# Layer 1's deferred steps: one in each tile of keys, in place of up to four ahead of each burst of weighted sums

## The chip, the cores and the metric

One core of a Trainium2 chip runs the whole program in one launch. The time is device microseconds of one execution, from the first instruction to the last; beside it the profiler's span of one profiled execution is given. Engines are named as the profile names them: PE is TensorE (matrix products), PEld its weight loads, DVE is VectorE, ACT is ScalarE, POOL is GpSimd, SP is the engine that issues most of the DMAs.

## The reference

Two layers, each a cross attention and a gated or routed feed-forward part, on x of 4 batches x 512 rows x 256 columns and a context of 4 x 1601 x 256, all in float32. The part that matters here is layer 1's attention, with 16 heads of 16 columns, and the routing that follows it:

```python
def _L1_xattn_ref(q, k, v, mask, wq_w, wq_b, wk_w, wk_b, wv_w, wv_b, fo_w, fo_b):
    qp = (q @ wq_w.T + wq_b).reshape(N, -1, HEADS, HEAD_DIM)
    kp = (k @ wk_w.T + wk_b).reshape(N, -1, HEADS, HEAD_DIM)
    vp = (v @ wv_w.T + wv_b).reshape(N, -1, HEADS, HEAD_DIM)
    energy = jnp.einsum('nqhd,nkhd->nhqk', qp, kp)
    energy = jnp.where(mask == 0, jnp.float32(-1e+20), energy)
    attention = jax.nn.softmax(energy / np.float32(np.sqrt(EMBED)), axis=3)
    out = jnp.einsum('nhql,nlhd->nqhd', attention, vp).reshape(N, -1, EMBED)
    return out @ fo_w.T + fo_b
...
x = x + _L1_xattn_ref(_layernorm(x, axis=-1), ctx_1024, ctx_1024, mask_Bx1xSxS2_ik1, ...)
x = x + _L1_ffn_ref(_layernorm(x, axis=-1), L1_ffn_gate_weight, L1_ffn_gate_up_proj, L1_ffn_down_proj)
```

The feed-forward part `_L1_ffn_ref` takes the softmax of 32 gate logits for each row, keeps the 8 largest, gives every row a place in the buffers of its 8 experts, and sums the experts' outputs by their shares.

## The kernel before, in words

The program runs layer 0 (`xattn0`, `ffn0`), then layer 1's attention (`xattn1_keys`, line 1150; another form, `xattn1`, is there for general masks and does not run with this input), then the experts (`experts1`). The change touches the attention and the norm that it shares with others.

**Slots and tiles.** `xattn1_keys` works through 16 slots (line 1404). A slot is one batch b and one group g of four heads. In a slot, the loop at line 1414 goes over NK = 13 tiles of 128 keys (the last has 65). For each tile and each of the four heads s, TensorE multiplies 128 keys with 512 queries (line 1428, tile `sb`, 32 rows of the array, row group s), and ScalarE takes the exponential into `pt` (line 1433).

**Maxima.** The scores need each query's maximum ahead of time. The generator `maxima` (line 1270) works one slot ahead: each `next(top)` runs `maximum` (line 1135), two products of 32 rows (line 1143, tile `sa`) into one of two double banks, and one VectorE reduction (line 1146, `mx`). The loop asks for 32/26 of them at every second head (lines 1419 to 1423). After the fourth maximum of a slot, `rows` (line 1288) transposes the slot's maxima and sends them to the row of `qs` that the scores read.

**Weighted sums.** The exponentials are kept in 23 buffers. After tiles 2, 5, 8, 10 and 12 the held tiles are put on a list, and two tiles later `burst` (line 1391) takes them off and calls `weigh` (line 1353): for each tile and head a product of the values with the exponentials, 32 columns of the array each, four heads side by side (line 1361). The sum is added into `ov` by VectorE (line 1369), or copied by ScalarE for the first (line 1367).

**Deferred steps.** All else is cut into steps by `yield` and waits on the list `more`; `step` (line 1297) runs the next piece of the list's first generator. They are:
- `project(b)` (line 1202): loads the context, takes the norm of x, adds the output's bias to x, then (after `yield True`) two steps of transposes, eight steps of key chunks (line 1223, stored to `kd` in memory through two buffers `kc`) and two of queries (line 1234, to `qd`).
- `values(b)` (line 1244): 13 steps, one for each tile of keys, of a product (line 1251) and a VectorE add into `v1` (line 1255).
- `normalise(i, ov)` (line 1306): transposes a slot's sums and divides them. It is put at the list's head when a slot's last burst has run.
- `finish(b)` (line 1325): the output projection in four steps, then the router's `route_steps` (line 1617): norm, transposes, logits, top 8, positions, and for each of four row tiles a step that builds one-hots (lines 1705 to 1718) and one that multiplies them (line 1725).

Before, a step is run in `burst` alone: up to four, ending early at a `yield True`, ahead of the weighted sums. Two other places run steps where something must be ready: line 1409 empties the list when batch 1 or 2 begins, and line 1276 runs steps until the projection that `maxima` needs is done.

**Banks and order.** Scores `sb`, the steps' products and the weighted sums all take turns in four PSUM banks (tag "s" of `ps_s`); the maxima have the other four, two pairs (`ps_a`). The order of the work on every engine is the order written (`tc.manual_schedule`, line 1371): an engine that waits holds back what is behind it.

**The norm.** `layernorm` (line 91) calls `moments` (line 95: eight VectorE instructions for four row tiles, and a square root on ScalarE) and `normed` (line 107: a reciprocal and four VectorE instructions). It is used by `project` and `route_steps`, where it ran as one piece.

## Time and profile before

| what | us |
|---|---|
| time, median of 3 runs (lowest, highest) | 2245.74 (2242.94, 2249.98) |
| the profiled execution's time | 2245.39 |
| its span | 2243.6 |
| layer 0, up to some 1003 us | about 1003 |
| layer 1's attention, first scores to the last weighted sum | 1008.3 to 1944.1 |
| routing of the last batch, then the experts | to the end |
| PE busy from 1100 to 1900, in each 100 us | 94 to 97 |
| DVE busy in the same stretches | 60 to 77 |
| ACT busy in the same stretches | 47 to 56 |
| weighted sums, 12 products of 512 columns (one burst of three tiles) | 2.71 |
| row work of tiles 1 to 3, 4 to 6, 7 to 9 in a slot without steps | 8.37, 7.52, 8.11 |
| VectorE reduction `mx`, mean | 0.989 |
| exponential `pt`, mean | 0.604 |

How to read it: the profile lists, for one execution, how long each engine was busy, in which stretches, and what ended each of its idle times. In a stretch's line the columns are its limits in us from the span's start, its length, and the busy time of PE, PEld, DVE, ACT and POOL with the number of instructions in brackets, then the TensorE clock that was granted (1.00 is full) and the load of the DMA engines. In a line of instructions, the count and the mean come after the shapes; what stands behind the last bar is the idle time of that engine just before them and who ended it.

### The profile page before, as it was taken

To read this page: it belongs to the slowest core of one execution; us is meant where nothing else is said; L and a number is where in the kernel's file an instruction comes from. 1 tells how busy PE (TensorE), PEld (TensorE's weight loads), DVE (VectorE), ACT (ScalarE), POOL (GpSimd) and SP (SyncE) were. 2 spreads that over 40 slices of the span, in tenths; PEclk is the share of its full clock that TensorE was granted. 3 is DMA by queue.
4 is the path that set the end of the run, shared out by engine and by line. 5 is a ranking of instruction groups with operands and counts; after the bars stand their busy time and mean duration, and the time that the engine had idled before them with its cause. 6 is when DMAs were issued, how large, how long until landed. Compare 5 with 4: busy or idle time off the path is not lost.

```text
span 2243.6 us, 29693 instructions
## 1 busy us (share of the span) xinstructions
PE 2069.1 (92%) x11446; PEld 1071.0 (48%) x11446; DVE 1183.3 (53%) x1916; ACT 736.0 (33%) x1543; POOL 772.4 (34%) x769
## 2 busy tenths in 40 slices
PE   6999999999999999989999999999999999859883
PEld 4677744444444543334444344444444444446551
DVE  5343346445555444656567667875677675232220
ACT  1221222112112121104545545554455555512121
POOL 9999445555444445531000000000000000037764
PEclk9999999999999999999999999999999999959996
DMA  6473121121122223133212222123122200037763
GB/s 212 134 257 101 44 78 48 49 64 50 51 61 68 57 73 75 53 66 70 72 33 35 69 47 47 29 57 66 28 37 33 42 11 11 19 107 184 166 146 38
DMA packets 98190, 161.89 MB, mean 72 GB/s; under 512 B 20100, under 2 KB 68760, under 8 KB 97528
## 3 DMA queue, kind: packets, MB, share of 16 engines
q1 hardware_dynamic: 79800, 126.00, 21.8%
q0 software_dynamic: 17664, 33.38, 7.3%
q8 instruction: 93, 1.52, 0.3%
q14 instruction: 57, 0.47, 0.1%
q10 hardware_dynamic: 576, 0.52, 0.1%
HBM read 137.28 MB, written 22.31 MB: 71 GB/s over the span
## 4 chain that ended last, share of the span: by engine, by line
PE 48%; DVE 8%; DMA 5%; issue 3%; POOL 1%; ACT 1%; POOLq 0%; ACTq 0%; SPq 0%; DVEq 0%
PE sb L1428 12%; PE sa L1143 10%; PE pv L1361 7%; DVE mx L1146 4%; DMA out<-eo,ids 4%; PE acc L561 3%; PE py L857 2%; PE pv L1251 2%; PE po_e L1507 2%; PE pk L1223 2%; PE gu L1491 1%; POOL out L1519 1%; PE pf L1342 1%; PE ph L1725 1%; DMA qd<-kc 1%
## 5 line engine op out<-in xcount | busy, mean ns | idle before, releaser
L1146 DVE TENSOR_REDUCE mx<-sa 128x2 f32<-128x802 f32 x512 | 494.5, 989 | 158.9 <-PE sb L1428 83.9
L1433 ACT ACTIVATE pt<-sb 128x512 f32<-128x512 f32 (+1 forms) x832 | 429.7, 605 | 277.2 <-PE sb L1428 253.0
L1143 PE MATMUL sa<-kq,qq 32*128 32x401 f32 x2048 | 475.0, 550 | 31.2 <-DVE mx L1146 25.2
L1143 PEld LDWEIGHTS sa<-kq,qq 32*128 32x128 f32 x2048 | 175.8, 189 | 202.1 <-DVE mx L1146 167.6
L1718 POOL TENSOR_TENSOR r_hold<-r_lb,r_pr 128x256 f32<-128x256 f32 x16 | 10.1, 629 | 684.1 <-DVE r_lb L1711 559.7
L1428 PE MATMUL sb<-b 32*128 32x512 f32 (+1 forms) x832 | 233.8, 657 | 10.5 <-ACT pt L1433 7.4
L561 PE MATMUL acc<-og,oe 128*128 128x512 f32 x512 | 239.7, 598 | 2.4 <-DVE og L542 2.4
L857 PE MATMUL py<-ve,xnT 128*128 128x512 f32 x512 | 231.7, 595 | 3.3 <-DVE mx L1146 3.2
L1428 PE MATMUL sb<-qs,ks 32*128 32x512 f32 (+1 forms) x832 | 226.2, 641 | 4.0 <-ACT pt L1433 3.5
L1361 PE MATMUL pv<-pt,v 128*32 128x512 f32 (+1 forms) x1664 | 196.1, 597 | 0.0
L862 DVE TENSOR_TENSOR y<-py,gm 128x1024 f32<-128x1024 f32 x64 | 78.3, 1224 | 209.2 <-PE py L857 152.4
L499 POOL TENSOR_SCALAR pr<-pr,den 128x128 f32<-128x128 f32 (+3 forms) x128 | 143.7, 1133 | 123.3 <-DVE den L497 123.3
L871 POOL TENSOR_TENSOR y_a<-y 128x512 f32<-128x512 f32 x64 | 81.5, 1273 | 247.7 <-DVE den L497 147.1
L488 ACT ACTIVATE pr<-sc,nm 128x128 f32<-128x128 f32 (+3 forms) x128 | 66.3, 523 | 280.1 <-DVE nm L484 177.8
L857 PEld LDWEIGHTS py<-ve,xnT 128*128 128x128 f32 x512 | 95.5, 190 | 118.0 <-issue 112.3
L561 PEld LDWEIGHTS acc<-og,oe 128*128 128x128 f32 x512 | 91.1, 190 | 90.3 <-issue 85.5
L1428 PEld LDWEIGHTS sb<-b 32*128 32x128 f32 (+1 forms) x832 | 89.2, 188 | 88.0 <-issue 34.3
L1428 PEld LDWEIGHTS sb<-qs,ks 32*128 32x128 f32 (+1 forms) x832 | 87.7, 182 | 81.7 <-issue 36.1
L1519 POOL DMA_INDIRECT out<-eo,ids x64 | 101.4, 1585 | 57.2 <-ACT eo L1513 36.7
L542 DVE TENSOR_TENSOR og<-gb,oT 128x512 f32<-128x512 f32 x128 | 114.6, 935 | 0.5
L1369 DVE TENSOR_TENSOR ov<-pv,ov 128x512 f32<-128x512 f32 x64 | 44.1, 688 | 121.2 <-PE pv L1361 120.5
L227 PE MATMUL sc<-ctxT,qT 128*128 128x512 f32 (+1 forms) x256 | 96.3, 527 | 7.3 <-ACT pr L239 7.3
(262 smaller groups left out, 2659.1 us busy)
## 6 DMA issues: line engine op xcount, KB each, us to landing
gb<-gd SPq DMA_DIRECT2D x128, 256.0 KB
mi<-in_mask POOLq DMA_DIRECT2D x32, 401.0 KB, 3.7
wgu<-in_E_gu SPq DMA_DIRECT2D x32, 384.0 KB
qq<-qd SPq DMA_DIRECT2D x64, 128.0 KB
kq<-kd SPq DMA_DIRECT2D x64, 100.2 KB
ctxT<-in_ctxT SPq DMA_DIRECT2D x8, 800.5 KB
ctxT<-in_ctxT SPq DMA_DIRECT2D x12, 512.0 KB
ctx<-in_ctx SPq DMA_DIRECT2D x12, 512.0 KB
```

The costliest lines, as they stand in the source:

```text
L227: nc.tensor.matmul(sc[:, c : c + n], qT[:, m, t * P : (t + 1) * P], ctxT[b][j][:, m, :n], start=(m == 0), stop=(m == 1),)
L499: nc.gpsimd.tensor_scalar(pr[:, j, :n], pr[:, j, :n], den[:, j : j + 1], None, ALU.mult)
L542: nc.vector.tensor_tensor(og, gb[:, i, :], oT[s], ALU.mult)
L561: nc.tensor.matmul(acc[b][m], oe[hp][:, c : c + P], og, start=(hp == 0 and e == 0), stop=(hp == NP - 1 and e == E0 - 1),)
L857: nc.tensor.matmul(py[:, j, :], xnT[:, k, t * P : (t + 1) * P], ve[:, k, j, :], start=(k == 0), stop=(k == 1),)
L871: nc.gpsimd.tensor_tensor(a, yy[:, :, :h4], yy[:, :, h4:], ALU.add)
L1143: nc.tensor.matmul(pa[:, j, :Q1], qq[r, s, t * P : (t + 1) * P], kq[r, s, :], start=True, stop=True)
L1146: nc.vector.tensor_reduce(mx[:, t, s, 2 * half : 2 * half + 2], pa[:, :, :Q1], AX.X, ALU.max)
L1361: nc.tensor.matmul(pv[32 * s : 32 * s + 32, :], v1[b % 2][:r, kt, h * VW : h * VW + 32], pts[s][:r, :], start=(kt == held[0][0]), stop=(kt ...
L1428: nc.tensor.matmul(sb[:r, :], ks[i % 2][q, kt * P : kt * P + r], qs[i % 2][q, :], start=True, stop=True,)
L1433: nc.scalar.activation(pt[:r, :], sb[:r, :], AF.Exp)
L1519: i = nc.gpsimd.indirect_dma_start(out=view, out_offset=bass.IndirectOffsetOnAxis(ap=router.ids[:, e, c : c + 1], axis=0), in_=eo[:, c, :] ...
```

## The change

The norm becomes a generator of four steps (`layernorm_steps`, `moments_steps`), used by `project` and `route_steps`; `moments` runs the same pieces at once for the other callers. `burst` no longer runs steps. In the loop over tiles, one step is run at the third head of every tile, after the maxima asked for there and ahead of that head's scores; a second one is run at the first head in every tile of slot 0 and in tile 1 of every other slot, ahead of the burst if one is due there. Steps that ended a burst's run of steps by `yield True` no longer differ from the others. The instructions and their operands stay as they were; their order changes.

```diff
--- before.py
+++ after.py
@@ -92,16 +92,38 @@
 
         return self.normed(b, pool, *self.moments(b, pool))
 
+    def layernorm_steps(self, b, pool, xn):
+
+        nc = self.nc
+        mv, rstd = yield from self.moments_steps(b, pool)
+        nc.vector.reciprocal(rstd, rstd)
+        xn.append(pool.tile([P, TB, D], F32, name="ln_xn"))
+        for t in range(TB):
+            self.normed_tile(b, t, xn[0], mv, rstd)
+            if t % 2:
+                yield
+
     def moments(self, b, pool):
 
+        steps = self.moments_steps(b, pool)
+        while True:
+            try:
+                next(steps)
+            except StopIteration as e:
+                return e.value
+
+    def moments_steps(self, b, pool):
         nc = self.nc
         mv = pool.tile([P, TB, 2], F32, name="ln_mv")
         for t in range(TB):
+            if t == 2:
+                yield
             st = pool.tile([P, 6], F32, name="ln_st")
             nc.vector.bn_stats(st, self.xs[b * TB + t])
             nc.vector.bn_aggr(mv[:, t, :], st)
         rstd = pool.tile([P, TB], F32, name="ln_rstd")
         nc.scalar.activation(rstd, mv[:, :, 1], AF.Sqrt, bias=self.eps)
+        yield
         return mv, rstd
 
     def normed(self, b, pool, mv, rstd):
@@ -109,11 +131,14 @@
         nc.vector.reciprocal(rstd, rstd)
         xn = pool.tile([P, TB, D], F32, name="ln_xn")
         for t in range(TB):
-            nc.vector.tensor_scalar(
-                xn[:, t, :], self.xs[b * TB + t], mv[:, t, 0:1], rstd[:, t : t + 1],
-                ALU.subtract, ALU.mult,
-            )
+            self.normed_tile(b, t, xn, mv, rstd)
         return xn
+
+    def normed_tile(self, b, t, xn, mv, rstd):
+        self.nc.vector.tensor_scalar(
+            xn[:, t, :], self.xs[b * TB + t], mv[:, t, 0:1], rstd[:, t : t + 1],
+            ALU.subtract, ALU.mult,
+        )
 
     def transposed(self, xn, pool, ps, tag):
 
@@ -1202,7 +1227,9 @@
             def project(b):
 
                 ctxT = ctx[b] = self.load_context(b, p1)
-                xn = self.layernorm(b, p1)
+                xn = []
+                yield from self.layernorm_steps(b, p1, xn)
+                (xn,) = xn
                 add_bias(b)
                 kd[b] = dram.tile([D, S2], F32, name="kd")
                 qd[b] = dram.tile([D, S], F32, name="qd")
@@ -1389,9 +1416,6 @@
                 ov = {}
 
                 def burst():
-                    for _ in range(4):
-                        if step():
-                            break
                     _, i, some = bursts.pop(0)
                     if some[0][0] == 0:
                         ov[i] = p2.tile([P, S], F32, name="ov")
@@ -1421,6 +1445,8 @@
                                 while due >= 1:
                                     next(top, None)
                                     due -= 1
+                            if s == 2 or (s == 0 and (i == 0 or kt == 1)):
+                                step()
                             if s == 0 and bursts and bursts[0][0] + 2 <= now:
                                 burst()
                             q = slice(32 * s, 32 * s + 32)
@@ -1618,7 +1644,9 @@
 
         nc, prog = self.nc, self.prog
         sh = [P, TB, E1]
-        xn = prog.layernorm(b, p1)
+        xn = []
+        yield from prog.layernorm_steps(b, p1, xn)
+        (xn,) = xn
         for t in range(b * TB, (b + 1) * TB):
             nc.sync.dma_start(prog.out[t * P : (t + 1) * P, :], prog.xs[t])
         nc.sync.dma_start(
```

## The prediction

> **What bounds the kernel now.** I read the page first, then stretches of the layer 1 attention cut at its slots (one slot is one batch and one group of four heads, 13 tiles of keys), then stretches cut where TensorE changes its kind of work, and last the order of time around one full-array product that already sits among the row-tiled ones.

> ```profile
> span 2243.6 us, 29693 instructions
> PE 2069.1 (92%) x11446; PEld 1071.0 (48%) x11446; DVE 1183.3 (53%) x1916; ACT 736.0 (33%) x1543; POOL 772.4 (34%) x769
> L1146 DVE TENSOR_REDUCE mx<-sa 128x2 f32<-128x802 f32 x512 | 494.5, 989 | 158.9 <-PE sb L1428 83.9
> L1433 ACT ACTIVATE pt<-sb 128x512 f32<-128x512 f32 (+1 forms) x832 | 429.7, 605 | 277.2 <-PE sb L1428 253.0
> ```

> The page: TensorE is busy nearly throughout, while VectorE's maxima (0.99 us each) and ScalarE's exponentials wait for it. A slot needs 32 maxima and 52 exponentials. "Busy" does not mean full: a row-tiled product uses a quarter of the array.

> ```profile
> core 0: us, PE busy (x) PEld busy (x) DVE busy (x) ACT busy (x) POOL busy (x), PEclk, DMA share, GB/s
> 1202.57:1250.95 48.38, 46.56 (x348) 19.63 (x344) 35.29 (x45) 28.76 (x55) 0.00 (x0) 1.00 0.23 35
> 1250.95:1328.76 77.81, 72.90 (x424) 34.59 (x420) 43.91 (x64) 35.11 (x65) 2.98 (x4) 0.96 0.27 67
> 1328.76:1391.77 63.01, 60.20 (x404) 29.43 (x401) 43.69 (x67) 32.26 (x61) 0.00 (x0) 0.97 0.22 42
> 1391.77:1446.34 54.57, 52.11 (x430) 22.76 (x427) 43.12 (x81) 29.02 (x56) 0.63 (x1) 0.97 0.17 30
> 1446.34:1496.99 50.65, 48.90 (x540) 22.55 (x536) 39.18 (x53) 30.27 (x58) 1.89 (x3) 1.00 0.21 33
> ```

> Five slots, the second column the length. The first is quiet: almost no deferred step runs in it, 48.38 us. The next four carry one batch's steps: keys and queries first (77.81), values (63.01), outputs and the router's norm (54.57), the rest of the routing (50.65). Their excess over quiet is 29.4 + 14.6 + 6.2 + 2.3 = 52.5 us per batch. This is what the change can win or lose; the quiet part stays.

> ```profile
> 1323.26:1326.91 3.65, 3.65 (x19) 2.96 (x17) 2.28 (x5) 0.98 (x3) 0.00 (x0) 1.00 0.01 1
> 1250.95:1265.57 14.62, 10.97 (x61) 5.35 (x57) 11.32 (x19) 8.53 (x15) 2.98 (x4) 0.77 0.26 104
> 1415.33:1424.44 9.11, 9.10 (x57) 4.53 (x53) 8.48 (x23) 5.56 (x11) 0.00 (x0) 1.00 0.10 25
> 1235.30:1241.49 6.19, 5.86 (x44) 2.84 (x40) 4.18 (x5) 3.94 (x8) 0.00 (x0) 1.00 0.65 67
> 1243.35:1249.10 5.75, 4.86 (x40) 2.42 (x37) 4.50 (x5) 3.12 (x7) 0.00 (x0) 1.00 0.33 88
> ```

> In order: four value steps in one burst (3.65 us, so 0.91 each); the row-tiled stretch in which a whole norm ran (8.37 in the quiet slot, so 6.25 more); the one in which the router's top-8 ran (8.11 quiet, so 1.0 more); and two stretches of two tiles each, the first with the transposes of the maxima (line 1291, called from line 1282) in its middle, the second without.

> ```profile
> 1238.51 0.60 PE L1291 MATMUL tp_m<-ident,nm 128*4 128x128 f32 x4
> 1239.03 1.43 PE L1428 MATMUL sb<-qs,ks 32*128 32x512 f32 x7
> 1239.99 0.52 PE L1143 MATMUL sa<-kq,qq 32*128 32x401 f32 x3
> 1240.88 1.89 DVE L1146 TENSOR_REDUCE mx<-sa 128x2 f32<-128x802 f32 x2 [1.27 <-PE sb L1428]
> ```

> That is a step of the kind that the change makes: full-array work alone among row-tiled work. It takes 0.53 us of TensorE's order (1238.51 to 1239.03), and VectorE then idles 1.27 us before its next maximum.

> **The change, part by part.** *What it moves.* Before, a burst ran up to four steps and then its weighted sums; five bursts a slot. After, a step runs at the second pair of heads of every tile, and one more in tile 1: 14 a slot, 26 in slot 0. One batch needs 17 (projection, its norm now four more) + 13 (values) + 4 (normalise) + 22 (outputs and routing, again four more) = 56 = 4 x 14, so the drain at line 1409 finds the queue empty and nothing piles up there. The number of products, copies and DMAs is unchanged. SP gets the same issues in nearly the same order; keys' stores come one per tile instead of four per burst.

> *Full-array steps* (52 values, 24 key chunks, 6 queries, 12 norm and router transposes and logits, 12 of the output: 106). In a burst each cost its TensorE time: stretches after stepped bursts are as long as after quiet ones (7.56 against 7.52 for tiles 4 to 6). Among row-tiled work, two score banks feed VectorE, and its maxima start 1.02 us apart (8 in 8.22 us): one maximum frees a bank, TensorE refills it in about 0.94 us, and the other maximum has then just ended. There is almost no slack, so a step that sits between two refills delays the next maximum by its own length. Bounds from the transposes above: 6.19 - 5.75 = 0.44 for 0.53 us, so 0.09 under par; VectorE's idle of 1.27 against its usual 0.14 is 1.13, so 0.6 over. The second is the nearer for a step whose following score products take the row groups that the next refill wants (the refill at 1239.99 starts when the second passes of 1239.57 end); by the count of 32/26 maxima per half tile this holds for every other step, and part is regained because both banks are then free. I take par, 0, with ends -0.09 x 106 = -10 and +0.6 x 106 = +64. The results' copies to SBUF fall into the idle time that the step makes, as they did in bursts.

> [...] The row: the first transpose starts 0.44 us after the last refill's second pass began, that is, at once when it has streamed, and the scores follow 0.2 us after the last transpose starts. [...]

> *VectorE's own steps.* Norms and routing have little TensorE work; in a burst VectorE did them while TensorE multiplied (2.48 of 2.71 us in the burst after the top-8), and now they stand in the chain of maxima. I charge each its time less 0.25 (maxima at 0.91 back to back instead of 1.02, 2.46 a tile), and nothing where the next thing is a burst.
> - The router's norm: 2 x (0.425 + 0.182) = 1.2, 1.2, 1.2 (reciprocal and two tiles at 0.51) and 1.0, less 1.0 = 3.6; ScalarE's square root with table loads of 1.28 there and back holds the exponentials, 1.5 of it felt: 5.1. Before, 2.8 (8.55 against 5.75). +2.3.
> - The projection's norm: 5.1 less 1.2, since its second piece stands just ahead of tile 1's burst: 3.9. Before 6.25. -2.3.
> - Top-8 and what goes with it: 4.2 (eight small ones a tile group, from 0.09 to 0.29) less 0.25 = 3.9; before 1.0. +2.9.
> - Slots and one-hots: 1.8 + 4 x (1.215 + 0.417) + 4 x 0.28 = 9.4; the two one-hots at tiles 9 and 11 go under bursts (-3.3), 1.2 off for seven steps; plus four small products at 0.6: 7.3. Before, 2.65 in its stretch and 4 x 0.62: 5.1. +2.2.

> Batches 1 and 2: +5.1 each. Batch 3 has routing alone (its norm cost 4.1 before, 10.25 against 6.19, and 4.5 now): +5.4. Batch 0 has a projection alone (4.1 before, 9.87 against 5.75, and 3.9 now): -0.2. Together +15. Ends: -5 if bursts go on hiding most of it, +35 if no burst hides any and ScalarE's stalls count whole.

> *Small parts.* Bursts with four key chunks waited for the two store buffers: 5.79 against 3 x 1.72 + 0.25 = 5.4, six times, -2; weighted sums waited for the last value's copy, 3.0 in all, -3. Normalise: its VectorE part (0.25 + 4 x 0.215 = 1.1) lay under the burst, now beside 0.59 of TensorE; +0.15 x 15 = +2. Start: the first value step stands ahead of the first scores (1008.3) and needs 1.6 MB of context whose issue begins at 1003.5; at the 355 to 384 GB/s of 1005 to 1009 that lands near 1009, the bias row later: +2 (0 to 4).

> Sum: 0 + 15 - 5 + 2 + 2 = +14 on the profiled execution's 2245.4 (span 2243.6 and 1.8 around it), which is the median of the runs, 2245.7, to 0.4 us. **2259 us.**

> **The rivals.** *Faster, 2217 us:* steps fill TensorE's waits for VectorE. For it: unhindered, TensorE issues a tile's row work in 1.85 us (1202.57 to 1204.42) where the tile takes 7.52 / 3 = 2.51; 0.66 is left a tile, and if 0.4 of it takes up step work in 106 tiles, that is 2245.4 + 14 - 42. Against: that slack is in pieces on single row groups, and a full-array product needs all four free. It decides from 0.13 us hidden per step. *Much slower, 2323:* every step meets the 0.6 us of the upper bound, +64 beside the +14; for it the 1.27 us of idle, against it the parity that frees every other step. *No change, 2245:* par for the products, and routing's VectorE work still hidden (end of -5 with +5 of the rest).

> **How the numbers follow.** The forecast (some 2252 to 2290) 0.44, much slower 0.14, no change 0.14, faster 0.28. Slower by over 0.3% (7 us, about what this kernel's measurement can tell): 0.44 + 0.14 = 0.58; within it 0.14; faster 0.28. The likeliest case's own range is 2252 to 2290; the range 2215 to 2305 reaches into both rivals so that about one in ten is left out on either side.

> **What would show it.** Right: slots with keys and values keep about 77 and 63 us, those with routing grow by some 5 in all, VectorE idles about 1 us after each step, and quiet slots stay at 48.4. Wrong: a tile with a value step takes under 3.2 us on average (2.5 + 0.9 less 0.2), so steps are hidden; or over 4, so row groups collide. If VectorE's wait for products falls while its busy time stays, the faster rival holds. The tail after the last slot (outputs and routing of batch 3) should not change at all.

## The result, and the profile after

The changed kernel takes 2310.48 us (median of 4 runs, 2306.66 to 2313.88) beside 2244.59 us before (4 runs): a ratio of 1.0289, 95% interval 1.0263 to 1.0315, some 65 us slower. I had forecast 2259 in a range of 2215 to 2305: the sign was right, the size was not, and the time lies outside the range.

The first view of the changed kernel's page is its head and the two groups shown of before:

```profile
span 2304.9 us, 29699 instructions
PE 2131.7 (92%) x11446; PEld 1073.4 (47%) x11446; DVE 1177.9 (51%) x1916; ACT 743.1 (32%) x1543; POOL 772.3 (34%) x769
L1171 DVE TENSOR_REDUCE mx<-sa 128x2 f32<-128x802 f32 x512 | 494.5, 989 | 264.6 <-PE sa L1168 144.6
L1459 ACT ACTIVATE pt<-sb 128x512 f32<-128x512 f32 (+1 forms) x832 | 438.1, 600 | 386.0 <-PE sb L1454 370.3
```

The counts of products, copies and reductions are those of before, and VectorE's busy time is 5 us less. What grew is waiting: the idle time ahead of the maxima from 158.9 to 264.6 us, ahead of the exponentials from 277.2 to 386.0, both for TensorE. And TensorE's own busy time grew by 62.6 us with the same 11446 products. Part of that is longer products: the times of all of them add up to 5626 us, before to 5556. Part is products that lie less side by side: in e7, below, the sum is 5556 again, and TensorE is still busy for 2100.4 us.

The span after less before is 61.3 us. Cut at the first score product of each slot (the first of all starts at 1009.4 us before, not at the 1008.3 given above), 4.5 us of it lie ahead of the first slot, 4.6 in batch 0's four slots, 16.5 in batch 1's, 20.1 in batch 2's, 17.2 in batch 3's, and -1.7 behind the last. Batch 1 in stretches, before (a cut some microseconds off the one in the prediction) and after:

```profile
core 0: us, PE busy (x) PEld busy (x) DVE busy (x) ACT busy (x) POOL busy (x), PEclk, DMA share, GB/s
1246.97:1321.12 74.15, 69.24 (x406) 31.63 (x404) 42.88 (x63) 35.96 (x65) 2.98 (x4) 0.95 0.29 73
1321.12:1385.40 64.28, 61.47 (x410) 30.74 (x408) 44.08 (x70) 32.15 (x61) 0.00 (x0) 1.00 0.19 36
1385.40:1440.46 55.06, 52.60 (x373) 23.32 (x371) 43.05 (x81) 28.88 (x56) 0.63 (x1) 0.97 0.22 37
1440.46:1493.00 52.54, 50.79 (x602) 23.64 (x600) 39.88 (x53) 29.66 (x58) 1.89 (x3) 0.97 0.19 27
```

```profile
core 0: us, PE busy (x) PEld busy (x) DVE busy (x) ACT busy (x) POOL busy (x), PEclk, DMA share, GB/s
1207.33:1256.06 48.73, 47.27 (x347) 20.21 (x345) 34.59 (x43) 28.16 (x54) 0.00 (x0) 1.00 0.21 32
1256.06:1319.63 63.57, 61.75 (x378) 23.75 (x375) 39.12 (x58) 34.02 (x61) 3.03 (x4) 1.00 0.27 64
1319.63:1385.38 65.75, 64.71 (x400) 27.82 (x396) 39.03 (x53) 29.66 (x57) 0.00 (x0) 1.00 0.23 44
1385.38:1446.91 61.53, 59.22 (x389) 27.24 (x386) 41.24 (x65) 33.78 (x63) 0.00 (x0) 1.00 0.19 38
1446.91:1518.61 71.70, 65.91 (x628) 29.43 (x625) 47.90 (x91) 29.70 (x58) 2.52 (x4) 0.86 0.17 27
```

The first line after is the quiet slot: 48.73, as it was. The next four sum to 262.55 where before they were 246.03. The keys' slot is shorter, since only 14 steps fit in it now and the rest slides into later slots; what was a routing slot of 52.54 us is one of 71.70, and its granted clock is 0.86.

The clock deserves its own view: the routing slot's pieces in the changed kernel. The first, third and fifth line are the 3.41 us ahead of a fall of the clock, the line behind each is the stretch that follows.

```profile
core 0: us, PE busy (x) PEld busy (x) DVE busy (x) ACT busy (x) POOL busy (x), PEclk, DMA share, GB/s
1460.49:1463.90 3.41, 0.97 (x5) 0.23 (x4) 3.03 (x20) 0.93 (x2) 0.00 (x0) 1.00 0.01 2
1463.90:1470.73 6.83, 6.45 (x29) 2.13 (x32) 4.35 (x8) 1.09 (x2) 0.00 (x0) 0.50 0.00 0
1477.56:1480.97 3.41, 2.18 (x16) 0.61 (x12) 3.41 (x5) 1.58 (x4) 0.63 (x1) 1.00 0.00 0
1480.97:1487.80 6.83, 6.83 (x86) 2.78 (x88) 2.46 (x4) 1.96 (x4) 0.00 (x0) 0.50 0.01 2
1491.21:1494.62 3.41, 2.38 (x14) 1.06 (x9) 3.31 (x5) 1.34 (x4) 0.63 (x1) 1.00 0.00 0
1494.62:1501.45 6.83, 6.72 (x89) 4.28 (x92) 3.74 (x6) 3.36 (x8) 0.00 (x0) 0.50 0.13 33
```

In the first, VectorE works 3.03 us on the top-8 and what goes with it while TensorE is busy 0.97; in the other two, VectorE has a one-hot step between two maxima, and TensorE is busy 2.18 and 2.38 of 3.41 us. After each of them the granted clock is 0.50 for 6.83 us, and TensorE is then the one that all wait for (VectorE is busy 4.35, 2.46 and 3.74 of 6.83). How a one-hot gets there is in the timeline of the second piece (start, length, engine, line; in brackets the wait ahead and its releaser):

```profile
1477.04 1.51 PE L1168 MATMUL sa<-kq,qq 32*128 32x401 f32 x6 [0.57 <-DVE mx L1171]
1477.81 1.21 DVE L1733 TENSOR_TENSOR r_ha<-r_hi,count 128x1024 f32<-128x1024 f32 x1
1478.94 0.42 DVE L1739 TENSOR_TENSOR r_lb<-r_lo,count 128x256 f32<-128x256 f32 x1
1479.27 1.88 DVE L1171 TENSOR_REDUCE mx<-sa 128x2 f32<-128x802 f32 x2
1479.39 0.51 ACT L1745 ACTIVATE r_hold<-r_lb,tok 128x256 f32<-128x256 f32 x1 [3.11 <-DVE r_lb L1739]
1480.31 1.07 PE L1168 MATMUL sa<-kq,qq 32*128 32x401 f32 x4 [1.23 <-DVE mx L1171]
1482.35 2.08 PE L1454 MATMUL sb<-qs,ks 32*128 32x512 f32 x4
1484.46 1.09 ACT L1459 ACTIVATE pt<-sb 128x512 f32<-128x512 f32 x2 [2.62 <-PE sb L1454]
1485.69 3.81 PE L1388 MATMUL pv<-pt,v 128*32 128x512 f32 x24
```

The one-hots (1.21 and 0.42 us) hold the next maxima back, so no bank comes free and TensorE waits 1.23 us for VectorE; ScalarE's copy of the one-hot waits 3.11 us and stands ahead of the exponentials. By the time that the scores come (1482.35), the clock is half: four of them take 2.08 us, the exponentials wait 2.62 us for them, and the burst that follows takes 3.75 us up to the next score product, where 2.71 is usual.

### The profile page after: what moved, and what is told of

Read it like the earlier page. It is cut to its first block, busy times and chain, and to the rows that moved or that the text cites. A ratio compares the mean times of both kernels' runs of the same rounds, so it can differ in the third digit from the quotient of the medians.

```text
span 2304.9 us, 29699 instructions
## 1 busy us (share of the span) xinstructions
PE 2131.7 (92%) x11446; PEld 1073.4 (47%) x11446; DVE 1177.9 (51%) x1916; ACT 743.1 (32%) x1543; POOL 772.3 (34%) x769
## 4 chain that ended last, share of the span: by engine, by line
PE 51%; DVE 6%; DMA 5%; issue 2%; POOL 1%; ACT 1%; POOLq 0%; SPq 0%; ACTq 0%; DVEq 0%
PE sb L1454 14%; PE sa L1168 10%; PE pv L1388 9%; DMA out<-eo,ids 4%; DVE mx L1171 3%; PE acc L586 3%; PE pv L1278 2%; PE py L882 2%; PE pk L1250 2%; PE po_e L1533 1%; PE gu L1517 1%; POOL out L1545 1%; PE pf L1369 1%; PE ph L1753 1%; DMA qd<-kc 1%
## 5 line engine op out<-in xcount | busy, mean ns | idle before, releaser
L1171 DVE TENSOR_REDUCE mx<-sa 128x2 f32<-128x802 f32 x512 | 494.5, 989 | 264.6 <-PE sa L1168 144.6
L1459 ACT ACTIVATE pt<-sb 128x512 f32<-128x512 f32 (+1 forms) x832 | 438.1, 600 | 386.0 <-PE sb L1454 370.3
L1168 PE MATMUL sa<-kq,qq 32*128 32x401 f32 x2048 | 467.6, 547 | 32.3 <-DVE mx L1171 27.5
L1168 PEld LDWEIGHTS sa<-kq,qq 32*128 32x128 f32 x2048 | 182.3, 190 | 173.3 <-DVE mx L1171 106.7
L1454 PE MATMUL sb<-qs,ks 32*128 32x512 f32 (+1 forms) x832 | 241.2, 667 | 0.0
L1388 PE MATMUL pv<-pt,v 128*32 128x512 f32 (+1 forms) x1664 | 207.4, 628 | 0.0
L1454 PEld LDWEIGHTS sb<-b 32*128 32x128 f32 (+1 forms) x832 | 83.5, 183 | 87.2 <-issue 42.0
L1388 PEld LDWEIGHTS pv<-pt,v 128*32 128x32 f32 (+1 forms) x1664 | 47.8, 114 | 134.6 <-issue 103.8
```

What stands on the lines that cost most here:

```text
L1168: nc.tensor.matmul(pa[:, j, :Q1], qq[r, s, t * P : (t + 1) * P], kq[r, s, :], start=True, stop=True)
L1171: nc.vector.tensor_reduce(mx[:, t, s, 2 * half : 2 * half + 2], pa[:, :, :Q1], AX.X, ALU.max)
L1388: nc.tensor.matmul(pv[32 * s : 32 * s + 32, :], v1[b % 2][:r, kt, h * VW : h * VW + 32], pts[s][:r, :], start=(kt == held[0][0]), stop=(kt ...
L1454: nc.tensor.matmul(sb[:r, :], ks[i % 2][q, kt * P : kt * P + r], qs[i % 2][q, :], start=True, stop=True,)
L1459: nc.scalar.activation(pt[:r, :], sb[:r, :], AF.Exp)
```

## The experiments

Fifteen kernels, each compared with runs of the kernel before on the same chip. "Half clock" is the time in the attention (first to last score product) for which the profiled execution was granted 0.50. That is one execution. "Withheld" is the mean over all runs of a kernel of (1 - mean granted clock) x span: the most that the clock can have cost over the whole program, since a product of the weighted sums takes 1.06 us at half clock where it takes 0.59 at full (medians in the changed kernel).

| kernel | median us | ratio to before, 95% interval | half clock, us | withheld, us |
|---|---|---|---|---|
| before | 2244 to 2250 | 1 | 45.6 | 85 to 90 |
| changed | 2310.5 | 1.0289 (1.0263, 1.0315) | 84.9 | 112 |
| e5: before, values alone | 2262.8 | 1.0079 (1.0059, 1.0099) | 63.9 | 90 |
| e9: before, values in fours | 2256.1 | 1.0050 (1.0036, 1.0064) | 50.1 | 92 |
| e8: before, projection's norm in four steps | 2240.6 | 0.9975 (0.9963, 0.9987) | 24.6 | 77 |
| e12: e8, projections alone | 2254.5 | 1.0038 (1.0025, 1.0052) | 41.7 | 86 |
| e10: e8, router's norm in four steps too | 2249.2 | 1.0014 (1.0002, 1.0025) | 33.8 | 82 |
| e11: e10 with unread products | 2261.5 | 1.0064 (1.0050, 1.0078) | 28.0 | 79 |
| e2: before, outputs and routing alone | 2302.3 | 1.0229 (1.0212, 1.0246) | 93.3 | 118 |
| e1: changed, outputs and routing in bursts | 2283.8 | 1.0142 (1.0122, 1.0162) | 54.3 | 90 |
| e7: the same with clean bursts | 2280.3 | 1.0154 (1.0134, 1.0175) | 44.9 | 87 |
| e15: changed, one-hots in bursts | 2269.8 | 1.0109 (1.0089, 1.0130) | 26.8 | 83 |
| e14: changed, top-8 in bursts | 2318.7 | 1.0321 (1.0303, 1.0338) | 91.7 | 113 |
| e3: changed with unread products | 2303.5 | 1.0240 (1.0222, 1.0257) | 26.3 | 87 |
| e13: the same, 128 columns wide | 2305.3 | 1.0255 (1.0238, 1.0273) | 51.0 | 99 |
| e6: changed, norms in one piece | 2338.6 | 1.0422 (1.0398, 1.0447) | 129.1 | 127 |
| e4: changed, no steps in the first two tiles | 2316.6 | 1.0289 (1.0272, 1.0306) | 87.4 | 112 |

Differences below are those of the ratios times 2245 us, since the medians come from different rounds.

### Which half: the projections and values, or the routing

*e1* leaves the changed kernel's steps in the tiles, but runs outputs and routing in the bursts:

```diff
                 def burst():
+                    for _ in range(4):
+                        if not is_late() or step():
+                            break
...
-                                step()
+                                if not is_late():
+                                    step()
```

> The changed kernel, but the steps of the output projection and of the routing go back into the bursts (up to four, ending at a step marked True) and the router's norm is one piece again; projections, values and normalise stay one in each tile. The changed kernel took 2310.5 us; cut at the first score of each slot, its slots 6, 7, 10, 11 and 13, where the routing runs, are longer than before by 6.4, 19.2, 6.3, 19.8 and 14.4 = 66 us, all other slots together by -7. Theory A (routing's VectorE work, one step a tile, stands in the chain of maxima and TensorE waits for it): most of the 66 goes, 2245 to 2262 us. Theory B (every full-array product alone among the row-tiled ones pays a drain and a lost overlap, the 0.6 us of my upper bound): routing holds few of the 106 such steps, so 2290 to 2310 us.

*e2* is the mirror: the kernel before, where only outputs and routing run one in each tile.

```diff
                     for _ in range(4):
-                        if step():
+                        if is_late() or step():
                             break
...
+                            if (s == 2 or (s == 0 and kt == 1)) and is_late():
+                                step()
```

> The other half: the kernel before, with its four steps to a burst for projections, values and normalise, but the output projection's and the routing's steps one in each tile (one more in tile 1), the router's norm in four pieces. Theory A: the loss comes with them, 2244.6 + 50 to 66 = 2295 to 2310 us. Theory B: 30 full-array steps at 0.2 to 0.6 us, 2251 to 2263 us.

e1 came 33 us under the changed kernel and 32 over before, between the two expectations: each half costs. e2 came 51 us over before, as theory A had it. The two do not add (32 + 51 is more than 65).

In e1 some work slid past its batch. *e7* starts from the kernel before, with the projections (their norm in four steps), values and normalising in tiles; a second step in each tile of the batch's second slot lets them end in time, so that outputs and routing stand in the bursts as before. Against e5, below, its core is:

```diff
-                            if s % 2 == 0 and now >= 2:
+                            if now >= 2 and (s == 2 or (s == 0 and (i == 0 or kt == 1 or (g == 1 and b)))):
                                 held_step(True)
```

> As e1_routing_in_bursts, but nothing of the routing can slip into a tile (in e1 the top-8 of each batch did) and none is left for a slot's start (in e1 three steps were): two steps a tile in each batch's second slot, none in the first two tiles of all. The router's norm is split, as in the changed kernel, but in a burst. e1 was at before + 34 us, and its slots 6, 7, 10 and 11 were 254 us against 214 before, partly by work that came later. If what slipped and was left (VectorE work in the open, and half clock behind it) is the cause: before + 8 to + 18. If the solo steps of projections and values alone make e1's 34: before + 25 to + 36.

(The router's norm is one piece there, as before, and not split as the expectation says.) +35 (30 to 39) over before at a half clock like before's (44.9 against 45.6; 87 us withheld against 85 in the same round): the price of steps alone, not of work that slid or of the clock. With the 5.6 us that the norm's four steps gain (e8, below) added back it is 40 us for 88 full-array steps and 15 of normalising, 0.39 each.

### The full-array steps alone

*e5* takes only the 52 value steps out of the bursts, two to a tile:

```diff
+                tiled = [more[0]]
...
+                            if s % 2 == 0 and now >= 2:
+                                held_step(True)
```

> The kernel before, but the 52 value steps (two products of 128x128 by 256 columns, one VectorE add each) run singly, two to a tile, from tile 2 of slot 0 on; all else stays in bursts. No VectorE-heavy step moves. Theory B (a full-array product by itself among row-tiled ones costs its time and a mode change): in the changed kernel four of them made slot 2 1.3 us longer, 0.33 each, so before + 17 us (+12 to +22). My par: before + 0 (-4 to +4). The range's lower side, hidden in TensorE's waits: before - 10 or less.

+18 (13 to 22), 0.34 us for each step, where I had put nothing. Up to 5 us of it can be the clock (90 us withheld, before 85 in the same round). But batch 1's four slots, with 13.7 us at half clock in both kernels, are 5.4 us longer for 13 value steps, so most of the price is not the clock's. *e9* runs them in fours:

```diff
-                            if s % 2 == 0 and now >= 2:
-                                held_step(True)
+                            if s == 2 and kt in (0, 3, 6, 9, 11) and now >= 2:
+                                for _ in range(4):
+                                    if held_step(True):
+                                        break
```

> The kernel before with the 52 value steps taken out of the bursts and put in fours into the middle of tiles 0, 3, 6, 9 and 11 (never just ahead of a burst of weighted sums): 16 interruptions of the row-tiled work (four a batch) in place of the 52 of the run with the values one by one, which cost 17 us over before, 0.33 each. The computation is whole. Theory A (the price is one of interruptions: the change of mode in and out, and the order of the score banks that it upsets): 16 x 0.33 = +5 us, 2248 to 2254. Theory B (the price belongs to each step, because its result is copied by VectorE in the chain of maxima): still about +17, 2258 to 2268. Theory C (being away from a burst of weighted sums is free once four go together): 2243 to 2247.

+11 (8 to 14), between A and B. e9 has 36 interruptions fewer than e5 and is 6.5 us shorter: 0.18 us each (0.03 to 0.33 by the two intervals). An interruption can be seen in the changed kernel: two value steps, each from its first product to the next score product,

```profile
1155.49:1156.55 1.06, 1.06 (x5) 0.68 (x4) 0.89 (x1) 0.82 (x2) 0.00 (x0) 1.00 0.54 130
1157.61:1158.67 1.06, 1.06 (x6) 0.68 (x5) 0.86 (x1) 0.96 (x2) 0.00 (x0) 1.00 0.00 0
```

1.06 us each, where the four in one burst took 3.65, or 0.91: 0.15 more. What e9's 11 us are does not show in the products, since a four takes 3.65 us there too (1348.24 to 1351.89):

```profile
1348.24 3.72 PE L1251 MATMUL pv<-w_X_wv,ctxT 128*128 128x256 f32 x16
1351.89 1.13 PE L1442 MATMUL sb<-qs,ks 32*128 32x512 f32 x4
```

Nor does it show where the fours run: in the profiled execution batches 1 and 2 are as long as before (0.0 and -0.2 us, with 3.4 us less at half clock in each), while slot 15, in which no such step runs, is 4.8 us longer with 10.2 us at half clock. So the price of a four by itself stays open; that singles cost more than fours is what the two runs show.

*e12* moves the projections (8 steps of key chunks, 2 of queries and 2 of transposes a batch, 36 in all) on top of e8, below:

```diff
-                tiled = [more[1]]
+                tiled = more[1:]
...
-                        tiled.append(more[-2])
+                        tiled.extend(more[-2:])
```

> The kernel before with the projection's norm in four steps of tiles, and now the projection's transposes, keys and queries one a tile as well (12 steps a batch, 36 in all); values, outputs and routing stay in bursts. The computation is whole. Base: the same without the projections moved, 0.9975 of before, about 2240. Theory A (a full-array step alone costs 0.33 us over par whatever it is): +12, 2249 to 2256. Theory B (a step of two 401-column products, which blocks all four row groups for 1.7 us, costs more, 0.6 as I bounded it): +22, 2258 to 2266. Par, as I forecast: 2238 to 2243.

+14 over e8, the size of theory A, but not its place. Of the 12.4 us between the two profiled executions 7.6 lie in slot 7: the routing slid, and the products of three one-hots were left when batch 2 began, where line 1409 of the kernel before runs what is left at once, with TensorE waiting,

```profile
1485.39 0.89 PE L1769 MATMUL ph<-r_hold,r_ha 128*32 128x16 f32 x64
1489.35 0.89 PE L1769 MATMUL ph<-r_hold,r_ha 128*32 128x16 f32 x64 [3.07 <-POOL r_hold L1762]
1493.06 1.05 PE L1769 MATMUL ph<-r_hold,r_ha 128*32 128x16 f32 x64 [2.82 <-POOL r_hold L1762]
```

and 6.6 lie in slot 15, in which no projection runs and 17.1 us are at half clock. So e12 gives no price of a projection's step.

### The norms

*e8* is the kernel before with one thing of the change, the projection's norm in four steps of tiles (the `yield True` behind the norm goes with it):

```diff
-                xn = self.layernorm(b, p1)
+                xn = []
+                yield from self.layernorm_steps(b, p1, xn)
...
+                            if s == 2 or (s == 0 and kt == 1):
+                                held_step(True)
```

> The kernel before with one thing changed: the norm ahead of each projection runs as four pieces, one a tile, in place of one piece ahead of tile 1's burst. Before, that piece made its stretch of row work 14.6 us where 8.4 is quiet, with the clock at half for 6.8 us. If pieces hide better: before - 4 to - 9 us (three norms). If VectorE's work costs the same wherever it stands in the chain: before - 2 to + 3.

-5.6 us (-3 to -8): faster than both kernels, and the only one of the fifteen that is. Its slot with the norm and the keys:

```profile
1244.27:1312.12 67.85, 65.82 (x395) 28.46 (x393) 40.45 (x60) 35.43 (x65) 3.02 (x4) 1.00 0.31 79
```

67.85 against 74.15 us, with the clock at 1.00 in place of 0.95. Most of this comes back, since three value steps and some of the outputs slid into the next slots: the four slots of batch 1 are 245.45 us against 246.03. Of the 7.2 us less between the two profiled executions, 2.8 lie in the batches with a projection's norm and 4.4 in batch 3, which has none. What the twelve runs do show is less clock withheld, 77 us against 85. *e10* treats the router's norm in the same way:

```diff
-                            more.append(finish(slots[i][0]))
+                            more.extend([finish(f), router_norm(f), route(f)])
+                            tiled.append(more[-2])
```

> The kernel before with both norms (the projection's and the router's) in four steps of tiles, and all full-array steps and the routing in bursts of up to four. The computation is whole. Base: the projection's norm alone so, 0.9975 of before, about 2240. Theory A (a norm split into tile steps is worth about 2 us each wherever it is, since a whole one stops the chain of maxima for 6 us): three more norms within the slots, 2233 to 2238. Theory B (the router's norm cost only 2.8 us in its burst, and in pieces it stands in the chain with ScalarE's square root): 2241 to 2249.

+9 over e8, theory B's size, but not its place. The routing slot of batch 1 is longer,

```profile
1436.45:1499.26 62.81, 55.69 (x624) 26.65 (x624) 47.20 (x89) 30.15 (x59) 2.51 (x4) 0.92 0.26 57
```

against 54.36 in e8, since here too the products of three one-hots were left for the start of batch 2 (1489.1 to 1497.8, 8.7 us). Batch 2, whose routing may run on into the next batch, is some 1.5 us shorter than in e8, and the rest of the difference lies ahead of the first scores and in slot 14. So the gain that theory A looked for isn't there, and the 9 us are no price of a norm. *e6* is the changed kernel with both norms in one piece, as before, but still in a tile:

```diff
-        xn = []
-        yield from prog.layernorm_steps(b, p1, xn)
-        (xn,) = xn
+        xn = prog.layernorm(b, p1)
```

> The changed kernel with both norms in one piece again (four steps fewer in each; everything else one step a tile). If the split helps (the projection's slots 4 and 8 got shorter by 10.6 and 7.8 us, of which 8.1 is work that moved to the next slot, so about 2 a projection): changed kernel + 3 to + 10 us. If the split costs (the router's norm, 2.3 each in my working, now four waits in place of one): changed kernel - 3 to - 10.

+30 over the changed kernel, three times what I expected at most. A whole norm stops the maxima for some six microseconds (5.9 in the trace of before, 1250.2 to 1256.1), and the half clock goes from 84.9 to 129.1 us, worth up to 22 of the 30 (by what was withheld in all runs, up to 15).

### The routing: top-8 and one-hots

*e14* puts only the top-8 back ahead of a burst, *e15* only the slots and one-hots (a flag that the routing sets at the step concerned):

```diff
                 def burst():
+                    for _ in range(4):
+                        if not router.in_bursts or step():
+                            break
...
-                                step()
+                                if not router.in_bursts:
+                                    step()
```

> The changed kernel with the top-8 alone (eight pairs of small VectorE operations and what goes with them) put back ahead of a burst; slots and one-hots stay in tiles. The computation is whole. Theory A (VectorE's top-8 stands in the chain and its wait sets off the first of the three stretches at half clock in each routing): 3 x (2.9 + 3.4) = 19 us under the changed kernel, 2288 to 2296, and one stretch of 6.8 us less in each routing. Theory B (the top-8 costs what I forecast and the clock falls for the one-hots all the same): 3 x 2.9 = 9 under, 2298 to 2306. If it is no matter where it stands: 2307 to 2314.

> The changed kernel with the slots and the four one-hots put back ahead of bursts, one one-hot a burst; the top-8 stays in a tile. The computation is whole; what the bursts of the slot do not reach runs at once at the next batch (some 4 us in two of the batches). Theory A (the one-hots' 1.6 us of VectorE each set off the second and third stretch at half clock): 3 x (6.8 + 2.2) - 8 = 19 under the changed kernel, 2286 to 2296, with one stretch of 6.8 us left in each routing. Theory B (the first stretch alone matters, the top-8's): 0 to 3 under, 2305 to 2314, with all three stretches still there.

e14 missed both its theories: +7 over the changed kernel. The top-8 ahead of a burst did not spare the fall of the clock (a stretch of 13.7 us at half clock from 1455.3, in place of 6.8 from 1463.9), and the one-hots behind it met other tiles. e15 came 40 us under the changed kernel, twice what theory A had. Slots 1 to 6 are as long as there, to 0.02 us; of the 36.9 us between the two profiled executions 34.6 lie in the three slots in which the one-hots run (7, 11 and 13). In the three routing slots the half clock went from 20.5 us each to 6.8, 6.8 and 3.4, as it said; over all runs 83 us are withheld in place of 112. Its routing slot of batch 1, and in it the tiles that answer to those of the timeline above, three tiles from one burst on (without the one-hot's products, 0.74 us from 1481.10), and the burst after them:

```profile
1447.67:1508.47 60.80, 57.09 (x629) 27.29 (x627) 48.19 (x91) 30.45 (x59) 2.51 (x4) 0.94 0.19 31
1472.79:1481.10 8.31, 7.92 (x56) 3.54 (x53) 6.88 (x8) 6.68 (x14) 0.63 (x1) 1.00 0.00 0
1481.84:1484.59 2.75, 2.75 (x38) 1.04 (x30) 2.15 (x4) 0.51 (x1) 0.46 (x1) 1.00 0.02 6
```

and the same of the changed kernel, with the one-hot and its products in the first line:

```profile
1472.02:1485.69 13.67, 11.87 (x120) 5.21 (x116) 8.96 (x17) 7.17 (x14) 0.63 (x1) 0.83 0.01 1
1485.69:1489.44 3.75, 3.75 (x27) 0.84 (x25) 0.99 (x1) 0.00 (x0) 0.00 (x0) 0.72 0.00 0
```

13.67 against 8.31 + 0.74 for the three tiles and 3.75 against 2.75 for the burst: 5.6 us more around one one-hot, which itself is 1.63 us of VectorE. In e15 the one-hot began under the burst ahead of these tiles (1472.32), and when it was done the next maximum still had to wait for TensorE,

```profile
1474.05 0.99 DVE L1171 TENSOR_REDUCE mx<-sa 128x2 f32<-128x802 f32 x1 [0.18 <-PE sb L1459]
```

so the maxima lost nothing.

### The clock by itself

*e3* adds to the changed kernel, in the routing of batches 0 to 2, eight full-array products of 512 columns that nothing reads: three behind the top-8, one behind the slots and one behind each one-hot.

```diff
+        def fill(n):
...
+            for _ in range(n):
+                nc.tensor.matmul(fl, prog.ident, xnT[:, 0, :], start=True, stop=True)
...
+        fill(3)
```

> The changed kernel with products that nobody reads added in the routing of batches 0 to 2: three of 128x128x512 after the top-8, one after the slots, one after each one-hot, 8 a batch at 0.86 us, 21 us of TensorE time in all. Of the 44 us more at half clock that the changed kernel shows between the first score and the end of the attention (92 against 48), most lies just behind these steps. Theory A with the clock as half of it (TensorE's waits there let the granted clock fall to 0.5, which doubles each product for 3.4 to 10 us): the fillers run in waits, the low stretches in slots 7, 11 and 13 shrink from about 20 us each, 2285 to 2303 us. Theory A by VectorE's chain alone: the clock's fall is a sign, not a cause; 2308 to 2330 us, longer by what of the 21 us finds no wait.

More work and 11 us less time: the half clock is 26.3 us in place of 84.9 (this profiled execution was the fastest of five, 2292.2 us; over all five 87 us are withheld in place of 112). In batch 1's routing slot,

```profile
1445.98:1513.87 67.89, 65.38 (x645) 28.22 (x642) 48.07 (x91) 29.67 (x58) 2.53 (x4) 0.97 0.17 28
```

67.89 us against 71.70, at a clock of 0.97 against 0.86. *e13* makes them 128 columns wide:

```diff
-                nc.tensor.matmul(fl, prog.ident, xnT[:, 0, :], start=True, stop=True)
+                nc.tensor.matmul(fl[:, :P], prog.ident, xnT[:, 0, :P], start=True, stop=True)
```

> The changed kernel with the same 24 unread products in the routing of batches 0 to 2, but 128 columns wide in place of 512 (some 5 us of TensorE work in place of 21; the computation is whole otherwise). The wide ones took 7 to 11 us off the changed kernel and left 26 us of the attention at half clock in place of 85. Theory A (the granted clock falls when TensorE has little to do over a stretch; each routing then has three stretches of 6.8 us at half clock, worth up to 3.4 us each, 30 us in all; the wide products cost about 20 of that): if narrow ones are enough to keep it up, 2283 to 2292; if the clock needs the work and not the presence, 2306 to 2315 with 60 us or more at half clock. Theory B (the half clock hardly costs, the wide products helped by their place): 2300 to 2306 with the half clock as it was.

It lies between theory A's two cases, 8 us under the changed kernel with 51.0 us at half clock: a quarter of the work spared 34 us of half clock where the whole spared 59. More work kept the clock up better here, though the narrow products too did more than half of it. *e11* asks the same of the routing in bursts, on e10:

```diff
+        fill(2)
         yield True
...
+            fill(1)
             yield True
```

> The same as the kernel with both norms in tile steps, and with unread full-array products in the routing of batches 0 to 2: two behind the top-8 and one behind each one-hot, 18 products of about 0.45 us, some 8 us of TensorE work that nothing reads. Theory A (the granted clock of TensorE falls when it waits for VectorE in the routing, and costs more than the products): 2 to 8 us under the kernel without them, and less than 20 us at half clock in the attention. Theory B (the clock matters only where the routing is in tile steps): 4 to 8 us longer than without.

+11 over e10, more than both theories had: where the routing runs in bursts, the products are only a cost. (I had written 0.45 us for a product; it is two instructions of 0.46, so the 18 are 16.6 us of TensorE, not 8.) The half clock fell by 5.8 us, worth up to 2.9, so as an estimate from one execution each the products cost some 14 of their 16.6, or 0.85 of their length. At that price e3's 24 cost 19 and gained 11 in all, so the clock was worth about 30 there; half of the 58.6 us that it spared is 29, and what was withheld fell by 25. That these agree is partly luck: of e11's loss 5.9 us lie in slot 15, which has one of the 18 products and 10.2 us at half clock.

### The start

*e4* leaves out the steps in the first two tiles, which wait for the context's load.

```diff
-                            if s == 2 or (s == 0 and (i == 0 or kt == 1)):
+                            if now >= 2 and (s == 2 or (s == 0 and (i == 0 or kt == 1))):
```

> The changed kernel, but no step in the first two tiles of slot 0. There the first value step waits for the context's 1.6 MB ahead of the first score, and slots 0 and 1 together with the later first score (1013.9 against 1009.4) lost 4.5 + 11.6 - 8.6 = 7.5 us. If that wait is the cause: 2302 to 2306 us. If the loss is the price of two steps a tile, which stay: 2308 to 2312 us.

No gain: the first scores come 3.8 us earlier (1010.1 against 1013.9), and slots 1 and 2 are 2.3 and 5.1 us longer.

## Why the prediction was wrong, by its steps

**Full-array steps at par: wrong, the first of the two terms that failed.** Measured 0.34 us a value step (e5) and 0.39 over the 103 steps of e7, so for all 106 some 36 to 41, in place of 0; the projection's steps by themselves were not measured. My ends were -10 and +64, so the cost had been bounded; what was wrong was to take par because a burst's steps cost par. The row that I set aside (VectorE idle 1.27 us after the transposes) was the better witness. "Every step meets the 0.6 us" was too much, by nearly half.

Why a step alone costs this was not shown: theory B of e1 names a drain, e5 and e9 a change of mode, and no run shows either. The runs show a price of going in and out, 0.18 us for each interruption by e5 and e9 (0.03 to 0.33) and 0.15 in the two windows, about half of e5's 0.34 a step.

**VectorE's own steps, +15: the second term that failed, in the line on slots and one-hots.** I had +2.2 in each of three routings, 6.6 in all; e15, which takes these steps back, is 40 us shorter, 13 a routing. I charged each VectorE operation its own length and stopped there. In the routing slot shown above, TensorE's wait for it is followed by a fall of the granted clock to 0.50, and the next 6.83 us of products, the burst with them, run at that clock (1.06 us for a product of the weighted sums in place of 0.59). Of e15's 40 us up to 29 are the clock's (half of the 58 us less, and as much by what was withheld), the rest the chain.

The other lines were not tested as cleanly. The projection's norm: I had -2.3 in each of two batches and -0.2 in the third, -4.8; e8 shows -5.6, which agrees in size, but what went is half clock, of which my working had nothing, and half of that (10 of 21 us) in batch 3, which has no such norm, so the agreement is partly luck. The router's norm: +2.3, +2.3 and +0.4; e10's +9 is mostly the one-hots left for the start of batch 2 and gives no price. The top-8, +2.9 a batch: not confirmed, since taking it back made the time 7 us longer.

Could it have been seen? The trace of before has it: the stretch of the whole norm that I showed has a clock of 0.77 in its line (1250.95 to 1265.57), and I read its 14.62 us without asking why. In the same trace, 1.07 us of TensorE work in 3.40 (1498.80 to 1502.20, another norm) stands ahead of 6.83 us at half clock.

**The small parts.** The normalise and store-buffer lines (+2 and -5) were not parted from the rest by any run; e7's 40 us have the normalising steps in them. The start, +2 (0 to 4): 4.5 ahead of the first scores, but with no gain from leaving it out.

**The rivals.** Faster: nothing hides, a value step costs 0.34. Much slower, 2323: nearest in time, 13 us away, but by its mechanism only about half is right; the other part, the clock, was in none of my cases. No change: excluded.

**What would show it.** Quiet slots 48.4 (48.73) and the tail (303.2 to 301.5 us behind the last score) held. That keys and values keep 77 and 63 us and routing grows by 5 did not: with 14 steps to a slot the work slides, and only a batch's sum can be compared.

**The account.** Changed less before is 65. 40 of them go when slots and one-hots return to the bursts (e15, up to 29 of it the clock). The other 25 (20 to 29) are what e15 is over before: all 106 full-array steps, both norms in pieces, normalising, the top-8 and a first score 5.3 us late. My sum had 6.6 for the first part and 7.4 for the second. That the second is under the 36 to 41 above is in part its clock: e15 has less half clock than before (26.8 against 45.6 us; 83 us withheld against 90), up to 7 to 9 us. Over the whole change the half clock of the attention grew by 39 us, worth up to 20; by what was withheld it is 22 to 27. The parts come from different bases and do not add exactly (e1 and e2 together are 18 too much): how steps alone and routing alone lean on each other, and why e14 was slower, stay open.

## What to carry to other kernels

Keep full-array steps in a group ahead of other work of their own kind: here one of the values took 0.91 us in a burst's group of four, and a step alone among row-tiled products was dearer by 0.34 (e5) to 0.39 us (e7). Small VectorE work like these one-hots belongs where TensorE has a long run of products of its own, as under a burst (e15, 40 us less; the top-8 ahead of a burst, in e14, gained nothing); where it stands in the chain that feeds TensorE, price the wait and then the products behind it at the clock that the trace shows there (0.50 for 6.83 us after each of the three waits above). Split only what stops that chain for longer than a tile (the whole norm: 5.6 us gained), and leave the rest: the part of the change that is worth having is that one. And when steps move, look at what slides behind them: the one-hots left for a batch's start cost e10 and e12 some 8 us each.

## What the runs showed of the hardware

```profile
1876.90:1880.30 3.40, 2.17 (x52) 0.77 (x49) 3.23 (x5) 2.22 (x5) 0.63 (x1) 1.00 0.00 0
1252.30:1255.70 3.40, 2.51 (x22) 1.13 (x20) 2.16 (x3) 2.04 (x4) 0.00 (x0) 1.00 0.20 47
```

So a window 0.64 busy has a fall behind it in one place (1477.56) and none in another; what else counts, no run settles.

And work that nobody reads can pay: 24 products of 0.92 us in the right places made the changed kernel 11 us faster.
